# A 16-state scan shares its products between VectorE and GpSimd, and its output projection goes by tokens

## The chip, the cores and the metric

The kernel runs on one core of one Trainium2 chip. The metric is the device time of a run in microseconds (us), lower is better. The five engines are called as the profile calls them: PE (TensorE, with PEld for its weight loads), DVE (VectorE), ACT (ScalarE), POOL (GpSimd) and SP (SyncE, which here issues the DMAs).

## The reference

The model has two layers on an image tensor x of 4 images x 128 channels x 64 x 64 pixels. Layer 0 is what the change touches. Cut to that part:

```python
# order: pixels sorted by the score of their 4x4 patch; x_re: x in that order, tokens of 128 channels
xz = layernorm(x_re + pe_re) @ in_proj_w.T           # 4096 tokens an image, 512 columns
xm, z = xz[..., :256], xz[..., 256:]
xc = silu(causal_conv4(xm) + conv1d_b)
dt_low, Bc, Cc = split(xc @ x_proj_w.T)              # 8, 16 and 16 columns
dt = softplus(dt_low @ dt_proj_w.T + dt_proj_b)
dA  = exp(dt[..., None] * A)                         # per token: 256 channels x 16 states
dBx = dt[..., None] * Bc[:, :, None, :] * xc[..., None]
def step(h, inp):                                    # over the 4096 tokens
    dA_t, dBx_t, C_t = inp
    h = dA_t * h + dBx_t
    return (h, einsum('bds,bs->bd', h, C_t))
y = (ys + D * xc) * silu(z)
out_m = y @ out_proj_w.T                             # back to 128 channels
x = x + out_m put back in the pixels' own order
```

Layer 1 is a scan with 256 states over the tokens (as they stand in the image, 8 chunks of 512 an image), and a spectral convolution. It reads layer 0's result and takes most of the time, but no instruction of it changes except from where it reads the projected tokens of the last image.

## The kernel before, in words

The kernel has three parts in time. `layer0_front` sorts the pixels and writes the normalised tokens, already in order, to DRAM (xnt), and the sorting permutation (permd). `layer0_scan` is the 16-state scan and ends with layer 0's result x2. `layer1` is the rest.

**Tiling of the scan.** An image's 4096 tokens are cut into 8 units of PJ = 512 tokens, so there are 32 units. The 256 channels are two halves (k) on 128 partitions, tokens run along the free dimension. A unit is scanned in two sub-blocks (i) of SUB = 256 tokens, and the 16 states in 8 pairs (g). One step j is one pair of states over one sub-block: a tile of 128 partitions x (2 states x 2 halves x 256 tokens) = 128x1024. There are 16 steps a unit and 512 in all. What is carried from a sub-block to the next is the last state of each of the rows (`last`), folded into the first token of the next sub-block's input.

**One step j** consists of these instructions, line numbers of the kernel before:

- `fetch` (L518): two DMAs on SP bring the rows of B and C for the two states, broadcast to 128 partitions (tile bc, named bcb in the profile; 6 buffers).
- `carry` (L527, every fourth step): POOL multiplies the first factor of the sub-block by `last`.
- `spread` (L532): POOL makes v = dx * B (128x1024), and L537 adds the carried value to the first token of v (128x4). v has 4 buffers.
- `lift` (L546): ACT makes the factors f = exp(dt * A) by four instructions, into one of two buffers in PSUM.
- `scan` (L554): DVE runs the recurrence over f and v and writes `states`, one buffer in PSUM. L558: DVE multiplies the states by C into p (3 buffers). L559: DVE copies the last states (128x4) to `last`.
- `add_up` (L570): PE adds p to y in PSUM by two matmuls with the identity; after the last pair of a sub-block, two matmuls with a diagonal matrix add D * xc (L576).
- `gated` (L586): once a sub-block, DVE multiplies y by silu(z) into yg.

**The order** is written by hand: no scheduler moves anything, and each engine runs its own instructions in the order in which the program names them. The loop over j stands at L632 to L649. In iteration j it issues fetch for step j+5, carry and spread for j+3, lift for j+1, the gate of step j-2 where a sub-block has ended there, scan of j with its product and copy, and add_up for j-1. So v is made three steps ahead of its scan, and f one step ahead.

**Work beside the steps.** `project` makes a unit's xz, dt, dx, and the B and C rows, which go through DRAM (bcd) to be broadcast; `output` projects a gated unit back to 128 channels; `put_back` sorts an image back and adds it to x. They are generators that yield after each piece: "mm" is a piece of matmuls that takes the one PSUM buffer `mm`, "post" the instruction that empties it, "free" a piece that needs no such buffer. `beside(j)` runs once an iteration, after add_up: at most one matmul piece holds the buffer at a time, and the projection goes ahead of the output. Projection of unit n starts when j reaches 16(n-1)-9, that is 25 steps before the unit's first scan.

**Output before.** A unit's 512 tokens are projected in four rounds (L457 to L468). Matmuls work on 32 rows at a time (every sixteenth token, so that a row is a patch), and ACT copies 32x512 into a tile `om` that holds a whole image in SBUF. After an image's last unit, `put_back` is queued behind the output and takes om back by matmuls with the permutation (L482), eight rounds, DVE adding each to the image tile xs (L488); xs holds half an image, loaded when that half begins, and is stored when it ends. The last image is not put back here: om goes to DRAM (omd, L655), and layer 1 puts it back at its beginning, reading omd at L989.

**Where layer 1 begins.** Its first loads (dlb, L1284, on SP) come behind the store of omd. Its scan (L1314, DVE) runs in place in SBUF over a ring buffer which POOL fills (L1298), with factors in PSUM from ACT (L1310).

Of the kernel before, what the change touches and what calls it, by code (L numbers as in the profile page):

```python
# [337 lines left out]
def layer0_scan(ctx: ExitStack, tc, ident, w, x, xnt, permd, x2, omd, psum, following):  # L338
# [111 lines left out]
    def output(b, unit, yg):  # L450

        if unit == 0:
            oms[b] = big.tile([128, 2, 16, 128], F32, tag="om", name="om", bufs=1)
        om = oms[b]
        yr = yg.rearrange("p k (r o) -> p k o r", o=16)
        rows = bass.ts(unit % 4, 32)
        for o in range(0, 16, 4):  # L457
            yield "mm"
            ps = middle()
            for i in range(4):  # L460
                for k in range(2):
                    nc.tensor.matmul(  # L462
                        ps[rows, bass.ts(i, 128)], yr[:, k, o + i, :], ow[:, k, :], start=k == 0, stop=k == 1
                    )
            yield "post"
            nc.scalar.copy(  # L466
                om[rows, unit // 4, o : o + 4, :], ps[rows].rearrange("p (i c) -> p i c", i=4)
            )  # L468

    def put_back(b):  # L470

        om = oms.pop(b)
        for h in range(2):
            xs = sm.tile([128, 8, 4, 64], F32, tag="xs", name="xs")
            cols = bass.ts(h, L // 2)
            nc.sync.dma_start(xs.rearrange("c py oy x -> c (py oy x)"), x[b][:, cols])
            for oy in range(4):
                yield "mm"
                ps = middle()
                for ox in range(4):  # L480
                    for r in range(2):
                        nc.tensor.matmul(  # L482
                            ps[:, bass.ts(ox, 128)], om[:, r, 4 * oy + ox, :], perm_t[:, b, r, bass.ts(h, 128)],
                            start=r == 0, stop=r == 1,
                        )
                yield "post"
                dst = xs[:, :, oy, :].rearrange("c py (px ox) -> c py px ox", ox=4)
                nc.vector.tensor_tensor(  # L488
                    dst, dst, ps.rearrange("c (ox py px) -> c py px ox", ox=4, px=16), ALU.add
                )  # L490
            nc.sync.dma_start(x2[b][:, cols], xs.rearrange("c py oy x -> c (py oy x)"))

# [11 lines left out]
    def tiles():  # L504
        return (
            big.tile([128, 4, PJ], F32, tag="xz", name="xz", bufs=3),
            big.tile([128, 2, PJ], F32, tag="dt", name="dt", bufs=3),
            big.tile([128, 2, PJ], F32, tag="dx", name="dx", bufs=3),
            big.tile([128, PJ // SUB, NS, 2], F32, tag="af", name="af"),
            dr.tile([2, NS, PJ], F32, tag="bcd", name="bcd"),  # L510
        )

    def fetch(j):
        n, i, g = place(j)
        bc = wk.tile([128, 2, 2, SUB], F32, tag="bc", name="bcb", bufs=6)
        src = ready[n][4][:, 2 * g : 2 * g + 2, bass.ts(i, SUB)]
        for q in range(2):
            nc.sync.dma_start(bc[:, q], src[q].partition_broadcast(128))  # L518
        return bc
# [9 lines left out]
    def spread(j, bc):  # L529
        n, i, g = place(j)  # L530
        v = wk.tile([128, 2, 2, SUB], F32, tag="v", name="v", bufs=4)
        nc.gpsimd.tensor_tensor(  # L532
            v, ready[n][2][:, :, bass.ts(i, SUB)].unsqueeze(1).broadcast_to((128, 2, 2, SUB)),
            bc[:, 0].unsqueeze(2).broadcast_to((128, 2, 2, SUB)), ALU.mult,
        )
        if units[n][1] or i:
            nc.gpsimd.tensor_tensor(  # L537
                v[:, :, :, 0], v[:, :, :, 0], ready[n][3][:, i, 2 * g : 2 * g + 2, :], ALU.add
            )
        return v  # L540
# [9 lines left out]

    def scan(j, v, bc):
        n, i, g = place(j)
        flat = "p n k t -> p (n k t)"
        nc.vector.tensor_tensor_scan(  # L554
            states.rearrange(flat), factors[j % 2].rearrange(flat), v.rearrange(flat), 0.0, ALU.mult, ALU.add
        )
        p = wk.tile([128, 2, 2, SUB], F32, tag="p", name="p")
        nc.vector.tensor_tensor(p, states, bc[:, 1].unsqueeze(2).broadcast_to((128, 2, 2, SUB)), ALU.mult)  # L558
        nc.vector.tensor_copy(last[:, 2 * g : 2 * g + 2, :], states[:, :, :, SUB - 1])  # L559
        return p  # L560
# [20 lines left out]
    def gated(j):  # L581
        n, i, g = place(j)
        if i == 0:
            ygs[n] = big.tile([128, 2, PJ], F32, tag="yg", name="yg")
        cols = bass.ts(i, SUB)
        nc.vector.tensor_tensor(ygs[n][:, :, cols], y.pop((n, i)), ready[n][0][:, 2:4, cols], ALU.mult)  # L586
        if i == PJ // SUB - 1:
            b, unit = units[n]
            behind.append(output(b, unit, ygs.pop(n)))
            if unit == L // PJ - 1 and b < NB - 1:  # L590
                behind.append(put_back(b))

# [7 lines left out]

    ready, ygs, oms, behind = {0: tiles()}, {}, {}, []
    for _ in project(*units[0], ready[0]):
        pass
    fronts, extra, rear, holder = [], [], None, None
    ahead = [1]

    def beside(j):
        nonlocal rear, holder
        if holder:
            keep = holder.kind == "hold"  # L610
            holder.next()
            holder = holder if keep else None
        if ahead[0] < len(units) and j >= per * (ahead[0] - 1) - 9:
            ready[ahead[0]] = tiles()
# [6 lines left out]
        if (rear is None or rear.kind is None) and behind:  # L621
            rear = Work(behind.pop(0))
        for work in (*fronts, rear, *extra):
            if work and work.kind == "free":
                work.next()
        for work in (*fronts, rear, *extra):
            if work and work.kind == "mm" and holder is None:
                work.next()
                holder = work

    bcs, vs, prods = {}, {}, {}
    for j in range(-9, steps):  # L632
# [8 lines left out]
        if j < 0:  # L641
            beside(j)
            continue
        if j >= 2 and (j - 2) % pairs == pairs - 1:
            gated(j - 2)
        prods[j] = scan(j, vs.pop(j), bcs.pop(j))
        if j:
            add_up(j - 1, prods.pop(j - 1))
        beside(j)  # L649
    add_up(steps - 1, prods.pop(steps - 1))  # L650
    gated(steps - 1)
    while holder or extra[0].kind or rear and rear.kind or behind:
        beside(steps)
    for h in range(2):
        nc.sync.dma_start(omd[h], oms[NB - 1][:, h])  # L655

# [249 lines left out]
def layer1(ctx: ExitStack, tc, ident, weights, work, psum, second, phi, pqd, mud, x, omd, permd, first, x2, x3, out):  # L906
# [43 lines left out]
    def put_back():  # L950
# [3 lines left out]
        for h in range(2):  # L954
            for oy in range(4):
                om = wide().rearrange("p r (i c) -> p r i c", i=4)
                for r in range(2):
                    nc.sync.dma_start(om[:, r], omd[r][:, bass.ts(oy, 4)])
                perm = small()[:, 0:256].rearrange("p (r j) -> p r j", r=2)
# [544 lines left out]
def conv_attn_hybrid(ctx: ExitStack, tc, w, out):  # L1504
# [13 lines left out]
    permd = dram.tile([128, NB, 2, 256], F32, name="permd")  # L1518
    omd = dram.tile([2, 128, 16, 128], F32, name="omd")
    layer0_front(tc, ident, half, w, x, xnt, permd, pqd, mud)  # L1520
# [55 lines left out]
```

## Time and profile before

The median of 3 runs is 21105.47 us (21103.82 to 21108.15).

| what | us |
|---|---|
| profiled execution, whole | 21106.96 |
| span from its first to its last instruction | 21105.0 |
| before the first scan of layer 0 | 614.8 |
| 16-state scan, first scan to last gate | 2066.5 |
| from there to layer 1's first scan | 29.2 |
| layer 1, from its first scan to the end | 18394.5 |

| engine | busy us in the span | share | instructions |
|---|---|---|---|
| PE | 17551.7 | 83% | 99112 |
| DVE | 20433.2 | 97% | 11824 |
| ACT | 15761.0 | 75% | 28195 |
| POOL | 19751.2 | 94% | 3541 |

How to read it: times are of one execution. A row of a group of instructions names the line, the engine, the operation, the tile written and the tiles read, partitions x elements, and the count; then the busy time of all and the mean of one in ns; then the time in which the engine sat idle just before them, and what ended most of that time. A row of a wait names who waited for whom, the total, how often, and the longest. In a list in order of time, the first number is the start in us from the beginning of the span and the second the duration. Durations of neighbours overlap slightly, so the distance between two starts is the better measure of what an instruction costs its queue. PE's ends are modelled.

### The profile page before, as it was taken

What the parts mean: (1) busy time and instruction counts of PE and PEld (TensorE: products, weight loads), DVE (VectorE), ACT (ScalarE), POOL (GpSimd) and SP (SyncE); (2) the same over time, 40 slices, a digit from 0 to 9 for tenths busy, and PEclk for the clock granted to TensorE, in tenths of its full rate; (3) what the DMA queues carried; (4) which work ended last, traced back from release to release, by engine and by line L of the source; (5) the groups of instructions that cost most, each with busy time, mean ns of one, the idle gap of its engine ahead of it and who ended that gap; (6) DMA issues with size and microseconds to landing.
All of it is one profiled execution on the core that took longest, in us unless ns stands there. A gap on an engine that the chain in (4) does not pass through costs nothing.

```text
span 21105.0 us, 282109 instructions
## 1 busy us (share of the span) xinstructions
PE 17551.7 (83%) x99112; PEld 7740.7 (37%) x99112; DVE 20433.2 (97%) x11824; ACT 15761.0 (75%) x28195; POOL 19751.2 (94%) x3541
## 2 busy tenths in 40 slices
PE   7788844655858888877868999599999999999998
PEld 4344421322323333343323344243434434434434
DVE  7799999999999999999999999999999999999997
ACT  3667667777777777777777777787887777788876
POOL 2666699999999999999999999999999999999997
PEclk8999966776979999998979999699999999999999
DMA  1555554555656666665656777577777777777775
GB/s 69 133 142 143 145 162 156 183 174 172 219 174 224 222 226 224 222 211 196 210 186 223 231 239 238 173 238 236 238 235 232 235 234 235 237 235 233 232 231 182
DMA packets 2194842, 4287.94 MB, mean 203 GB/s; under 512 B 768744, under 2 KB 1288208, under 8 KB 1928080
## 3 DMA queue, kind: packets, MB, share of 16 engines
q1 hardware_dynamic: 2193424, 4269.90, 63.3%
q8 instruction: 784, 12.85, 0.2%
q14 instruction: 634, 5.19, 0.1%
HBM read 3645.09 MB, written 623.91 MB: 202 GB/s over the span
## 4 chain that ended last, share of the span: by engine, by line
DVE 51%; issue 15%; PE 12%; POOL 5%; ACT 4%; DMA 1%; DVEq 0%; SPq 0%; POOLq 0%; ACTq 0%
DVE ring L1314 49%; PE conv L1257 6%; POOL ring L1298 4%; PE yp L1344 3%; ACT da L1310 2%; PE fin L1199 1%; ACT conved L1269 1%; DMA strip<-in_phi 0%; ACT t L804 0%; PE mm L883 0%; PE mm L877 0%; PE mm L868 0%; PE mm L1039 0%; PE conv L1111 0%; ACT ye L1351 0%
## 5 line engine op out<-in xcount | busy, mean ns | idle before, releaser
L1298 POOL TENSOR_TENSOR ring<-u,dlb 128x4088 f32<-128x4088 f32 x2048 | 18075.4, 8889 | 67.4 <-DMA dlb<-delta 37.7
L1314 DVE TENSOR_TENSOR_SCAN ring<-da,ring 128x1024 f32<-128x1024 f32 x8192 | 17927.7, 2263 | 180.4 <-ACT da L1310 149.6
L1310 ACT ACTIVATE da<-dlb,at 128x511 f32<-128x511 f32 x16384 | 11321.1, 691 | 4049.2 <-DVE ring L1314 3763.3
L1257 PE MATMUL conv<-strip,tok 128*128 128x512 f32 (+3 forms) x20224 | 8569.6, 551 | 46.0 <-DMA strip<-in_phi 45.0
L1344 PE MATMUL yp<-ring,c 128*32 128x256 f32 x65536 | 4917.1, 428 | 2493.9 <-DVE ring L1314 1283.8
L1257 PEld LDWEIGHTS conv<-strip,tok 128*128 128x128 f32 x20224 | 3606.1, 191 | 4105.8 <-issue 3722.3
L1344 PEld LDWEIGHTS yp<-ring,c 128*32 128x32 f32 x65536 | 2007.5, 119 | 6188.5 <-issue 3468.9
L532 POOL TENSOR_TENSOR v<-dx,bcb 128x1024 f32<-128x1024 f32 x512 | 1208.8, 2361 | 633.0 <-DVE states L554 629.4
L1199 PE MATMUL fin<-conved,pq 128*128 128x512 f32 (+1 forms) x3840 | 1750.5, 549 | 9.2 <-ACT sum L1220 4.8
L546 ACT ACTIVATE f<-dt,an 128x255 f32<-128x255 f32 x2048 | 974.7, 476 | 493.0 <-DVE states L554 442.3
L554 DVE TENSOR_TENSOR_SCAN states<-f,v 128x1024 f32<-128x1024 f32 x512 | 1176.0, 2297 | 106.3 <-ACT f L546 54.7
L1351 ACT COPY ye<-yp 128x512 f32<-128x512 f32 x2048 | 1185.9, 579 | 24.5 <-PE yp L1344 23.4
L570 PE MATMUL y<-p,ident 128*128 128x512 f32 x2048 | 1008.6, 618 | 173.5 <-DVE p L558 170.0
L1269 ACT COPY conved<-conv 128x512 f32<-128x512 f32 x1664 | 963.0, 579 | 146.3 <-PE conv L1257 143.2
L1199 PEld LDWEIGHTS fin<-conved,pq 128*128 128x128 f32 x3840 | 644.5, 192 | 385.8 <-issue 278.0
L558 DVE TENSOR_TENSOR p<-states,bcb 128x1024 f32<-128x1024 f32 x512 | 627.0, 1225 | 38.3 <-DVE states L554 0.5
L570 PEld LDWEIGHTS y<-p,ident 128*128 128x128 f32 x2048 | 363.6, 193 | 709.1 <-issue 336.8
L1304 ACT COPY ring<-vf 128x8 f32<-128x8 f32 x2048 | 386.8, 189 | 4.1 <-DMA omd<-om 4.1
L462 PE MATMUL mm<-ow,yg 128*32 128x128 f32 x2048 | 250.8, 276 | 39.2 <-ACT om L466 37.7
L462 PEld LDWEIGHTS mm<-ow,yg 128*32 128x32 f32 x2048 | 219.3, 133 | 136.4 <-ACT om L466 60.8
L1357 ACT COPY last<-ring 128x8 f32<-128x8 f32 x1792 | 267.2, 198 | 0.0
L407 PE MATMUL mm<-xin,taps 128*128 128x512 f32 x512 | 236.4, 605 | 23.2 <-DVE f L384 20.0
(242 smaller groups left out, 5484.3 us busy)
## 6 DMA issues: line engine op xcount, KB each, us to landing
dlb<-delta SPq DMA_DIRECT2D x2048, 1024.0 KB, 5.3
strip<-in_phi SPq DMA_DIRECT2D x1536, 448.0 KB, 5.0
yd<-ye SPq DMA_DIRECT2D x2048, 256.0 KB, 4.6
bcb<-bcd SPq DMA_DIRECT2D x1024, 256.0 KB, 4.3
strip<-in_phi SPq DMA_DIRECT2D x1024, 256.0 KB, 4.9
pq<-pqd SPq DMA_DIRECT2D x1408, 64.0 KB, 4.4
yt<-yd SPq DMA_DIRECT2D x4096, 4.0 KB, 4.4
pq<-pqd SPq DMA_DIRECT2D x256, 128.0 KB, 4.2
```

The lines of the kernel that those rows point to most:

```text
L532: nc.gpsimd.tensor_tensor(v, ready[n][2][:, :, bass.ts(i, SUB)].unsqueeze(1).broadcast_to((128, 2, 2, SUB)), bc[:, 0].unsqueeze(2).broadca ...
L546: nc.scalar.activation(factors[j % 2][:, a, k, 1:], ready[n][1][:, k, SUB * i + 1 : SUB * i + SUB], AF.Exp, scale=an[:, k, 2 * g + a : 2 * ...
L554: nc.vector.tensor_tensor_scan(states.rearrange(flat), factors[j % 2].rearrange(flat), v.rearrange(flat), 0.0, ALU.mult, ALU.add)
L570: nc.tensor.matmul(t.rearrange("p k t -> p (k t)"), ident, p[:, a].rearrange("p k t -> p (k t)"), start=g == 0 and a == 0, stop=False, ski ...
L1199: nc.tensor.matmul(fin[:, bass.ds(c0, w)], pq[:, n, :], u[:, bass.ds(c0, w)], start=begin and n == 0, stop=end and not partly, skip_group_ ...
L1257: nc.tensor.matmul(ps[:, skip:], tok[:, 1 - r if side else r, j, :], strip[:, bass.ds(c0 - lo, TS - skip)], start=which == 0 and j == js[0 ...
L1269: nc.scalar.copy(u[:, cols], ps[:, cols])
L1298: nc.gpsimd.tensor_tensor(ring[:, q % NQ, :, :, 1:], ready[0][:, :, 1:].unsqueeze(1).broadcast_to((128, VD, 2, TS - 1)), dl[:, :, 1:].unsq ...
L1310: nc.scalar.activation(da[:, h, 1:], dl[:, d % VD, 1:], AF.Exp, scale=at[:, h, d : d + 1])
L1314: nc.vector.tensor_tensor_scan(v, da.rearrange("p h t -> p (h t)"), v, 0.0, ALU.mult, ALU.add)
L1344: nc.tensor.matmul(yp[i // 2][bass.ts(p, 32), i % 2], c[:, h, t], moving(h, 128 * i + 32 * p, 32), start=h == 0, stop=h == 1,)
L1351: nc.scalar.copy(ye, yp[j].rearrange("p i d t -> p i t d"))
```

## The change

All of it lies in `layer0_scan`, apart from a shape of omd.

- On 5 of 16 steps (pairs 1, 3, 5 of a unit's first sub-block and 1, 4 of its second) the step is "shared": the scan runs in place in v in SBUF, and one iteration later POOL copies its last states and makes its product with C, into a tile of its own (pp, 2 buffers). PE adds such a product three iterations after its scan instead of one. The other 11 steps are as before.
- In an iteration, POOL's queue now holds carry and v for j+3, then the copy and product of a shared j-1. The gate of j-2 moves from before the scan of j to after it and its product.
- bc has 8 buffers instead of 6, v 6 instead of 4, af and bcd 3 instead of 2.
- `output` takes a unit in one round: four groups of 128 tokens, 128x128 each, one ACT copy of 128x512 to a tile ot, and one store to omd in DRAM, which now holds all four images. om no longer stays in SBUF.
- `put_back` is a queue of its own beside the output, and takes the image in eight pieces; image rows and projected tokens of the next piece are loaded one piece ahead, and each piece is stored at once.
- A unit's projection starts 29 steps before its first scan instead of 25.
- Layer 1 reads omd[b, r] for the last image.

```diff
     def output(b, unit, yg):
-        if unit == 0:
-            oms[b] = big.tile([128, 2, 16, 128], F32, tag="om", name="om", bufs=1)
-        om = oms[b]
-        yr = yg.rearrange("p k (r o) -> p k o r", o=16)
-        rows = bass.ts(unit % 4, 32)
-        for o in range(0, 16, 4):
+        yield "mm"
+        ps = middle()
+        for i in range(PJ // 128):
+            for k in range(2):
+                nc.tensor.matmul(
+                    ps[:, bass.ts(i, 128)], yg[:, k, bass.ts(i, 128)], ow[:, k, :], start=k == 0, stop=k == 1
+                )
+        yield "post"
+        ot = sm.tile([128, PJ // 128, 128], F32, tag="ot", name="ot", bufs=2)
+        nc.scalar.copy(ot, ps.rearrange("p (i c) -> p i c", c=128))
+        rows = omd[b].rearrange("h r o c -> (h r o) c")[bass.ts(unit, PJ)]
+        nc.sync.dma_start(rows.rearrange("(i p) c -> p i c", p=128), ot)
...
+        def load(i):
+            h, oy = divmod(i, 4)
+            xs = sm.tile([128, 8, 64], F32, tag="xs", name="xs", bufs=2)
+            nc.sync.dma_start(xs, image(x, h, oy))
+            om = sm.tile([128, 2, 4, 128], F32, tag="om", name="om", bufs=2)
+            for r in range(2):
+                nc.sync.dma_start(om[:, r], omd[b, r][:, bass.ts(oy, 4)])
+            return xs, om
...
+    def shared(j):
+        n, i, g = place(j)
+        return g in ((1, 3, 5), (1, 4))[i]
+
-    def scan(j, v, bc):
+    def scan(j, v):
         n, i, g = place(j)
         flat = "p n k t -> p (n k t)"
+        h = v if shared(j) else states
         nc.vector.tensor_tensor_scan(
-            states.rearrange(flat), factors[j % 2].rearrange(flat), v.rearrange(flat), 0.0, ALU.mult, ALU.add
+            h.rearrange(flat), factors[j % 2].rearrange(flat), v.rearrange(flat), 0.0, ALU.mult, ALU.add
         )
-        p = wk.tile([128, 2, 2, SUB], F32, tag="p", name="p")
-        nc.vector.tensor_tensor(p, states, bc[:, 1].unsqueeze(2).broadcast_to((128, 2, 2, SUB)), ALU.mult)
-        nc.vector.tensor_copy(last[:, 2 * g : 2 * g + 2, :], states[:, :, :, SUB - 1])
+        return h
+
+    def keep(j, h):
+        n, i, g = place(j)
+        engine = nc.gpsimd if shared(j) else nc.vector
+        engine.tensor_copy(last[:, 2 * g : 2 * g + 2, :], h[:, :, :, SUB - 1])
+
+    def product(j, h, bc):
+        mine = shared(j)
+        p = wk.tile([128, 2, 2, SUB], F32, tag="pp" if mine else "p", name="p", bufs=2 if mine else 3)
+        engine = nc.gpsimd if mine else nc.vector
+        engine.tensor_tensor(p, h, bc[:, 1].unsqueeze(2).broadcast_to((128, 2, 2, SUB)), ALU.mult)
         return p
...
-        if ahead[0] < len(units) and j >= per * (ahead[0] - 1) - 9:
+        if ahead[0] < len(units) and j >= per * (ahead[0] - 1) - 13:
...
+        if j and shared(j - 1):
+            h = states_of.pop(j - 1)
+            keep(j - 1, h)
+            prods[j - 1] = product(j - 1, h, bcs.pop(j - 1))
+        h = scan(j, vs.pop(j))
+        if shared(j):
+            states_of[j] = h
+        else:
+            prods[j] = product(j, h, bcs.pop(j))
+            keep(j, h)
         if j >= 2 and (j - 2) % pairs == pairs - 1:
             gated(j - 2)
-        prods[j] = scan(j, vs.pop(j), bcs.pop(j))
-        if j:
+        if j >= 3 and shared(j - 3):
+            add_up(j - 3, prods.pop(j - 3))
+        if j and not shared(j - 1):
             add_up(j - 1, prods.pop(j - 1))
         beside(j)
```

## The prediction

> **What bounds the kernel now.** I read the page first, for where the time lies; then the busy time of each engine in the stretches between the layers; then the groups of instructions and the waits inside the layer-0 scan; and last single instructions in order of time, because what is to be added up is the distance between two starts and not the recorded durations, which overlap a little.
>
> The stretches (busy us of each engine, count of instructions, granted clock, DMA share, GB/s):
>
> ```profile
> 614.80:2681.30 2066.50, 1740.04 (x5561) 836.47 (x5560) 1890.43 (x1638) 1438.98 (x2712) 1387.11 (x1141) 0.98 0.54 141
> 2681.30:2710.50 29.20, 7.81 (x64) 6.86 (x64) 0.87 (x5) 5.20 (x9) 9.15 (x3) 0.73 0.36 144
> 2710.50:21000.00 18289.50, 15290.10 (x91936) 6595.91 (x91936) 18119.91 (x9036) 14074.61 (x25036) 18213.22 (x2283) 0.92 0.66 215
> ```
>
> The columns of busy time are PE, PE's weight load, DVE, ACT, POOL. The 16-state scan is the first stretch: 2066.5 us from its first scan to its last gate. DVE is busy 1890 of it, POOL only 1387. The third stretch is layer 1: POOL is busy in 18213 of 18290 us there and the change leaves its instructions alone, so I keep it as it is and only shift it. The gain or loss is made in the first two stretches.
>
> Inside the first stretch (count | busy us, mean ns | idle just before, releaser):
>
> ```profile
> L532 POOL TENSOR_TENSOR v<-dx,bcb 128x1024 f32<-128x1024 f32 x508 | 1199.5, 2361 | 632.9 <-DVE states L554 629.4 <-DMA bcb<-bcd 3.6
> L554 DVE TENSOR_TENSOR_SCAN states<-f,v 128x1024 f32<-128x1024 f32 x512 | 1176.0, 2297 | 106.3 <-ACT f L546 54.7
> L558 DVE TENSOR_TENSOR p<-states,bcb 128x1024 f32<-128x1024 f32 x512 | 627.0, 1225 | 38.3 <-DVE states L554 0.5
> L537 POOL TENSOR_TENSOR v<-v,af 128x4 f32<-128x4 f32 x480 | 96.9, 202 | 37.6
> L559 DVE COPY last<-states 128x4 f32<-128x4 f32 x512 | 77.6, 152 | 0.0
> DVE yg L586 <- PE y L576: 54.8, 38, 2.9
> DVE states L554 <- ACT f L546: 54.7, 33, 48.2
> DVE xs L488 <- DMA xs<-in_x: 23.7, 6, 7.6
> ```
>
> POOL's idle time is 633 us and ends with DVE's scan; DVE's own idle time is small: 55 us for y, 24 us for the image tile, and 6.5 us for f (48.2 of the 54.7 is the one wait at the start). So DVE sets the pace of this stage and POOL waits for it. One step, in order of time (start us, duration us), and POOL back to back, and layer 1's scan:
>
> ```profile
> 698.07 2.30 DVE L554 TENSOR_TENSOR_SCAN states<-f,v 128x1024 f32<-128x1024 f32 x1
> 700.46 1.22 DVE L558 TENSOR_TENSOR p<-states,bcb 128x1024 f32<-128x1024 f32 x1
> 701.60 0.15 DVE L559 COPY last<-states 128x4 f32<-128x4 f32 x1
> 701.88 2.30 DVE L554 TENSOR_TENSOR_SCAN states<-f,v 128x1024 f32<-128x1024 f32 x1
> ...
> 1002.89 2.35 POOL L441 TENSOR_TENSOR dx<-dt,xz 128x1024 f32<-128x1024 f32 x1
> 1005.20 2.35 POOL L532 TENSOR_TENSOR v<-dx,bcb 128x1024 f32<-128x1024 f32 x1
> 1007.63 0.20 POOL L537 TENSOR_TENSOR v<-v,af 128x4 f32<-128x4 f32 x1
> 1007.82 2.37 POOL L532 TENSOR_TENSOR v<-dx,bcb 128x1024 f32<-128x1024 f32 x1
> ...
> 5020.25 17.55 DVE L1314 TENSOR_TENSOR_SCAN ring<-da,ring 128x1024 f32<-128x1024 f32 x8
> ```
>
> A DVE step costs 3.81 us: 2.39 scan, 1.14 product, 0.28 copy. The sum for the stage now: 512 x 3.81 = 1951; 64 gates, each putting 0.66 in the place of 0.28, 24; 24 image additions at 0.59, 14; idle 86. Together 2075 against 2066 measured, 0.4% over.
>
> **The change, part by part.**
>
> *DVE loses 160 products and 160 copies* (5 of 16 steps, 32 units). A shared step leaves only its scan, which now runs in place in v. Layer 1 has the same scan (factors in PSUM, 1024 elements in place in SBUF): 17.55/8 = 2.19 us from start to start. New DVE sum: 352 x 3.81 = 1341; 160 x 2.19 = 350; 64 gates now behind a shared scan at 0.59, 38; image additions 14; total 1743 us before waits.
>
> *POOL gains them.* The product has no row on POOL, but v (L532) has the same shape, two SBUF inputs, one of them broadcast: 2.31 us from start to start when nothing depends on it (dx at 1002.89 to v at 1005.20), 2.44 when the next instruction reads it. I take 2.33; the ends are 2.31 and 2.44. The copy of 128x4 has no POOL row either; nearest is L537 of the same size at 0.20; the ends are DVE's 0.15 and 0.35. Nothing excludes that it is cheaper than I take it; at no cost at all it is 32 us less. POOL's queue for all units from the first shared product on (v 0 to 5 are made ahead in the six buffers while DVE waits for its first f): 480 v with their addition at 2.61 (1005.20 to 1007.82) = 1253; 26 without it at 2.31 = 60; 120 carries at 0.20 = 24; 31 dx at 2.31 = 72; 160 products at 2.33 = 373; 160 copies at 0.20 = 32. Total 1814 us, 70 more than DVE's 1743. **POOL becomes the bound of the stage**, at about 57.3 us a unit instead of 64.4.
>
> Here the Trainium skill speaks against the edit: "GPSIMD Engine Reference", section 4.1, wants elementwise work on VectorE, since a two-input operation is about twice as slow on GpSimd. The rows agree on the price (2361 against 1225 ns, 1.93 times). By the rule alone the move adds 160 x 1.14 = 181 us of engine time, and a kernel whose engines took turns would end near 21290. But these two run side by side and POOL has 633 us to spare in this stage, so the longer queue decides, not the sum.
>
> *Waits that the change adds.* (1) POOL's copy and product of step j-1 stand behind v of step j+3 and wait for scan j-1; behind them stand the next v, which DVE needs three steps later. With POOL as the bound DVE has by then got to about step j+2, so it may lag by some three steps (10 us) before POOL waits. (2) PE adds a shared product two steps later (j-3 in iteration j); behind it stand the next additions and the projection's matmuls, for which ACT's copies, then f behind them, then DVE wait. When POOL is just in time, the product of group 5 is ready 2.5 us after scan 9 starts, and two additions (1.8 each) and the diagonal pair (0.9) make the gate wait until about 7 us after that start, where DVE would be there after 2.2: a stall of up to 4.7 us twice a unit. It makes DVE lag, and the lag makes the next such stall shorter; DVE has 70 us over the stage, 2.2 a unit, for it. (3) SP's new stores of ot wait for ACT, the image loads for the store of the tile before (now up to 5.3 us at one load); behind them stand the fetches of bc, which with eight buffers are issued some four steps before POOL uses them (14 us, landing takes 4.3). I take 0.3 us a unit, 10 us, for all POOL waits; the ends are 0 and 2 us a unit (64).
>
> *Waits that go.* The gate stands behind one more scan (2.2 us; the longest of the 54.8 us of waits was 2.9), and image tiles are loaded ahead (23.7 us). Both were on DVE, which no longer bounds, so they are worth nothing by themselves; without them DVE's sum would be too close to POOL's.
>
> *Output projection:* per unit 16 records of 128x128 in place of 64 (a batch of 16 takes 1.9 us either way, L462 and L482), one copy in place of four (0.58 each), one more store of 256 KB, and 32 loads and stores an image in place of 4. PE and ACT have room (1740 and 1439 of 2066). It shows only at the end: now four rounds of matmul and copy, 2.63 us apart, stand between the last gate and the store that layer 1's first load waits for; one is left: 3 x 2.63 = 7.9 us less.
>
> *29 instead of 25 steps ahead:* silu with its two table loads (4.5 us of ACT) now falls on step 10 of 16, where the steps around it are full ones; there ACT's f was late by 0.17 us in the trace, and I count 1 us a unit of DVE's lag, hidden under POOL.
>
> **The sum.** The first shared scan ends 6.2 us after the first scan starts (3.81 + 2.39, at 614.8), so POOL's queue runs from 621 to 2435 if it never waits. The last v is ready 2.5 us earlier, at 2432; from the last scan's start to the gate it is 6.56 us as now (2674.68 to 2681.24), and one more product in PE's queue adds some 2: gate at 2440.5 instead of 2681.2, 241 less. With 8 less behind it and 10 for POOL's waits: 239 us. The span goes from 21105.0 to 20866, the profiled execution from 21106.96 to 20868; the median of the runs, 21105.47, is 1.5 us below it: **20866 us**, 1.1% faster.
>
> **Rivals.**
>
> *Waits between the engines eat a part.* For it: two queues within 4% of each other, joined by PE in order and by ACT's two buffers of f. Against it: three steps of slack each way. At 2 to 3 us a unit on POOL instead of 0.3, 54 to 86 us: 20920 to 20952.
>
> *POOL is quicker than summed and DVE bounds.* DVE's 1743 plus 20 to 40 us of waits would put the last gate at 2378 to 2398, 303 to 283 earlier than now: 20794 to 20814 with the 8 at the end. It needs POOL's product and copy at no more than 2.3 us together, and v's rows say 2.53.
>
> *Slower: the in-place scan locks POOL out.* The Trainium skill, "SBUF — State Buffer", section "The single rule", gives DVE and GpSimd a shared port that one of them holds for the whole instruction. Shared scans now write SBUF instead of PSUM; if POOL stood still for each, 160 x 2.19 = 350 us would be added to the bounding queue: 21105 - 239 + 350 = 21216. It decides from 239/160 = 1.5 us a shared step. Against it stand layer 1's rows: the same scan in SBUF at 2.19 us beside a POOL that is busy 99.6% of that stretch, at 8889 ns for 4088 elements, 2.17 ns each, where v in this stage has 2361/1024 = 2.31. The page too counts inputs from SBUF, and the scan has one of its two in PSUM.
>
> *The change doesn't do what it says* (POOL's product ends up waiting for DVE each time, and the pace stays 3.81 a step) would give about 21097, only the 8 us at the end. The code puts v three steps ahead of it, so I give it little.
>
> **Chances and range.** As summed: 0.62, with its own range 20845 to 20890 (copy 0.15 to 0.3, product 2.31 to 2.44, POOL waits 0 to 0.7 us a unit). Waits eat a part: 0.21. DVE bounds: 0.09. No change: 0.02. Slower: 0.06. What a measurement can tell from no change is 0.2%, 42 us, so the first three are faster: 0.92; same 0.02; slower 0.06. For 8 in 10 I leave out the slower cases, the upper end of the waits and the last of the DVE case: 20825 to 20945.
>
> **What would show it.** POOL busy over 95% of the scan stage, and its idle time no longer for DVE's scan; DVE's scan waiting for POOL's addition to v (L546 of the new kernel) instead; POOL's product at 2.3 to 2.4 us and its copy near 0.2; the shared scans at 2.2 to 2.3; a unit of 57 to 58 us; the stage some 240 us shorter, and layer 1 as long as it is (18394 us from its first scan to the end). Wrong would be: POOL's v or product longer than 2.5 us beside the in-place scans, POOL idle for DVE, PE or ACT by more than 2 us a unit, or a longer layer 1.

## The result and the profile after

The changed kernel takes 21222.28 us (median of 4 runs, 21218.0 to 21234.8) against 21105.26 us before: a ratio of 1.0056, 95% interval 1.0044 to 1.0069. It is **slower by 117 us** where 239 us less were predicted. The profiled execution took 21220.3 us, its span 21218.5.

The stretches of the changed kernel, cut as before: first scan to last gate, last gate to layer 1's first work, layer 1 (start:end, length, then busy us and count of PE, PE's weight load, DVE, ACT, POOL, the granted clock, DMA share, GB/s):

```profile
608.20:2805.80 2197.60, 1687.88 (x4076) 756.99 (x4076) 1667.04 (x1318) 1387.64 (x2619) 1758.28 (x1460) 0.88 0.50 142
2805.80:2835.00 29.20, 1.86 (x16) 1.59 (x14) 11.55 (x9) 9.12 (x15) 19.81 (x4) 0.62 0.39 153
2835.00:21100.00 18265.00, 15292.08 (x91904) 6598.85 (x91904) 18096.91 (x9027) 14061.63 (x25016) 18198.74 (x2282) 0.92 0.66 216
```

The scan stage takes 2197.6 us instead of 2066.5: 131.1 more. It begins 6.6 us earlier (608.2), and layer 1's first scan comes 18.5 us behind the last gate instead of 29.2, so 10.7 less. From that scan to the end it is 18394.2 us, as before (18394.5). 131.1 - 6.6 - 10.7 = 113.8, which is the difference of the two spans within 0.3. So all of the loss is in the scan stage, and there no engine bounds any more: outside its recorded work DVE has 531 us and POOL 439.

The groups of that stretch (count | busy us, mean ns of one | idle of the engine just before them, releasers):

```profile
L541 POOL TENSOR_TENSOR v<-dx,bcb 128x1024 f32<-128x1024 f32 x507 | 1193.0, 2354 | 165.2 <-DMA bcb<-bcd 165.0
L568 DVE TENSOR_TENSOR_SCAN states<-f,v 128x1024 f32<-128x1024 f32 x352 | 807.5, 2294 | 312.7 <-ACT f L555 272.4 <-POOL v L541 18.1 <-POOL last L576 2.8
L582 POOL TENSOR_TENSOR p<-v,bcb 128x1024 f32<-128x1024 f32 x160 | 375.9, 2350 | 0.0
L568 DVE TENSOR_TENSOR_SCAN v<-f,v 128x1024 f32<-128x1024 f32 x160 | 365.0, 2281 | 89.6 <-ACT f L555 80.6 <-POOL v L546 6.1 <-POOL af L536 2.9
L576 POOL COPY last<-v 128x4 f32<-128x4 f32 x160 | 30.2, 189 | 80.9 <-DVE v L568 80.9
```

The prices were right: POOL's product 2350 ns, its copy 189, the scan in place 2281, and v no slower than before (2354 against 2361). What is new is the third column: DVE waits for ACT's factors f (272.4 + 80.6 us, where it was 54.7). The waits of the same stretch (total us, times, longest; "SPq" is the DMA queue of SP):

```profile
DVE states L568 <- ACT f L555: 272.4, 96, 46.3
ACT xz L412 <- PE mm L407: 204.8, 58, 11.9
POOL v L541 <- DMA bcb<-bcd: 165.0, 89, 10.1
PE mm L407 <- DMA xin<-xnt: 155.6, 27, 11.0
DVE yg L609 <- PE y L599: 125.7, 31, 4.3
POOL dx L441 <- ACT dt L439: 91.1, 30, 4.0
DVE v L568 <- ACT f L555: 80.6, 28, 3.0
...
SPq L428 <- ACT bc L427: 524.1, 31, 17.5
SPq L463 <- ACT f L555: 275.2, 30, 12.2
```

Read from below, they are a chain. SP stands for ACT before it may store the projected tokens (L463; the row names f, but in the unit below the store leaves at 2077.49, just as ACT's copy of 2076.88 ends). PE's convolution taps (L407) then wait for the projection's input xin, ACT's xz (L412) for those taps, f stands behind xz on ACT, and DVE waits for f. Before, the taps waited for xin for 0.9 us in the whole stage. One unit in order of time (start us, duration, and in brackets the idle time of the engine before it and its releaser; SP, then PE, ACT, DVE):

```profile
2077.49 0.36 SPq L463 DMA_DIRECT2D omd<-ot  x1
...
2079.03 0.45 SPq L399 DMA_DIRECT2D xin<-xnt  x1
...
2074.89 1.95 PE L456 MATMUL mm<-ow,yg 128*128 128x128 f32 x16
2076.68 3.60 PE L593 MATMUL y<-p,ident 128*128 128x512 f32 x8
2086.06 5.14 PE L407 MATMUL mm<-xin,taps 128*128 128x512 f32 x8 [5.79 <-DMA xin<-xnt]
2094.48 3.60 PE L407 MATMUL mm<-xin,taps 128*128 128x512 f32 x8
...
2076.88 0.59 ACT L461 COPY ot<-mm 128x512 f32<-128x512 f32 x1 [2.40 <-PE mm L456]
2091.24 0.69 ACT L412 ACTIVATE xz<-mm,cb 128x512 f32<-128x512 f32 x1 [3.92 <-PE mm L407]
...
2093.92 2.30 DVE L568 TENSOR_TENSOR_SCAN states<-f,v 128x1024 f32<-128x1024 f32 x1 [1.25 <-ACT f L555]
2104.12 0.69 DVE L609 TENSOR_TENSOR yg<-y,xz 128x512 f32<-128x512 f32 x1 [4.33 <-PE y L599]
```

The output's matmuls at 2074.89 feed ACT's copy at 2076.88; its store leaves SP at 2077.49, and only behind it can xin be issued (2079.03) of a projection whose matmuls PE has next. PE has nothing to do for 5.79 us, and the eight taps after that gap take 5.14 us instead of 3.60. The next additions to y start that much later, and the gate at 2104.12 waits 4.33 us for them. With 29 steps a projection begins one iteration behind the output's store; with 25 it begins five behind it.

From every second gate to the next (the second of each unit) it was 62.4 to 63.9 us before in a unit with nothing of put_back beside it. After, most are 66 to 69 (the first ones up to 71.9), those with put_back up to 78.4, and the last two, which have no projection of layer 0 left beside them, 56.5 and 50.5. POOL's predicted 57.3 us is reached only there.

### The profile page after: what moved, and what is told of

It reads as the page before. It is cut to its first block, busy times and chain, and to the rows that moved or that the text cites. A ratio compares the mean times of both kernels' runs of the same rounds, so it can differ in the third digit from the quotient of the medians.

```text
span 21218.5 us, 278713 instructions
## 1 busy us (share of the span) xinstructions
PE 17494.9 (82%) x97576; PEld 7657.8 (36%) x97576; DVE 20208.9 (95%) x11504; ACT 15707.8 (74%) x28099; POOL 20123.7 (95%) x3861
## 4 chain that ended last, share of the span: by engine, by line
DVE 52%; issue 15%; PE 12%; ACT 4%; POOL 4%; DMA 1%; DVEq 0%; SPq 0%; POOLq 0%; ACTq 0%
DVE ring L1348 51%; PE conv L1291 6%; POOL ring L1332 3%; PE yp L1378 3%; ACT da L1344 2%; PE fin L1233 1%; ACT conved L1303 1%; DMA strip<-in_phi 0%; PE mm L911 0%; PE mm L902 0%; ACT t L838 0%; PE conv L1145 0%; ACT ye L1385 0%; PE mm L1073 0%; PE mm L917 0%
## 5 line engine op out<-in xcount | busy, mean ns | idle before, releaser
L541 POOL TENSOR_TENSOR v<-dx,bcb 128x1024 f32<-128x1024 f32 x512 | 1204.6, 2354 | 165.3 <-DMA bcb<-bcd 165.0
L593 PE MATMUL y<-p,ident 128*128 128x512 f32 x2048 | 1047.8, 656 | 201.6 <-DVE p L582 110.3
L568 DVE TENSOR_TENSOR_SCAN states<-f,v 128x1024 f32<-128x1024 f32 x352 | 807.5, 2294 | 312.7 <-ACT f L555 272.4
L593 PEld LDWEIGHTS y<-p,ident 128*128 128x128 f32 x2048 | 406.6, 206 | 761.1 <-issue 473.1
L582 DVE TENSOR_TENSOR p<-states,bcb 128x1024 f32<-128x1024 f32 x352 | 431.0, 1224 | 24.0 <-DVE states L568 0.4
L568 DVE TENSOR_TENSOR_SCAN v<-f,v 128x1024 f32<-128x1024 f32 x160 | 365.0, 2281 | 89.6 <-ACT f L555 80.6
L407 PE MATMUL mm<-xin,taps 128*128 128x512 f32 x512 | 287.5, 714 | 191.4 <-DMA xin<-xnt 175.3
L582 POOL TENSOR_TENSOR p<-v,bcb 128x1024 f32<-128x1024 f32 x160 | 375.9, 2350 | 0.0
L441 POOL TENSOR_TENSOR dx<-dt,xz 128x1024 f32<-128x1024 f32 x32 | 75.2, 2349 | 245.6 <-ACT dt L439 245.6
```

Source lines behind the costliest of these rows:

```text
L541: nc.gpsimd.tensor_tensor(v, ready[n][2][:, :, bass.ts(i, SUB)].unsqueeze(1).broadcast_to((128, 2, 2, SUB)), bc[:, 0].unsqueeze(2).broadca ...
L568: nc.vector.tensor_tensor_scan(h.rearrange(flat), factors[j % 2].rearrange(flat), v.rearrange(flat), 0.0, ALU.mult, ALU.add)
L593: nc.tensor.matmul(t.rearrange("p k t -> p (k t)"), ident, p[:, a].rearrange("p k t -> p (k t)"), start=g == 0 and a == 0, stop=False, ski ...
```

## The experiments

Each kernel was run in a batch beside the kernel before (21100.46, 21105.08 and 21102.26 us for the three batches). All but the last are single runs. Several runs of one kernel spread over 12 us (before) to 28 us (the last experiment), so smaller differences count only where a line of the trace stands beside them. Theory A puts the loss on the projection's new place among the in-order queues; its rival B on the shared steps and the coupling of DVE and POOL.

**e1_noshare: no step is shared**, everything else as after.

```diff
     def shared(j):
-        return g in ((1, 3, 5), (1, 4))[i]
+        return False
```

> The changed kernel with no shared step: all products and copies are DVE's again; output by tokens, the place of the projection 29 steps ahead, the buffers and the moved gate stay. Theory A (the new placement and the new store close a ring of in-order queues: the unit's input xin is loaded by SP behind the store of ot, which waits for ACT's copy, which waits for PE; PE then stands idle for xin, ACT behind PE, DVE behind ACT's f): PE still waits for xin, over 60 us in all, but a full step of 3.81 us leaves ACT slack, so 21060 to 21150. Theory B (the shared steps take the slack that silu and softplus on ACT need, wherever the projection stands): without sharing no stall is left, 62.4 us a unit, 21020 to 21050, and PE's wait for xin costs nothing.

21183.13 us. Outside of both ranges, but the loss stays without a shared step: 83 us slower than before, ordinary units mostly of 65 to 68 us. PE waits 96.3 us for xin and POOL 440 us for bc. That speaks against B as the cause, and says that at 29 steps sharing costs 39 us more.

**e2_place25: the projection starts 25 steps ahead as before**, everything else as after.

```diff
-        if ahead[0] < len(units) and j >= per * (ahead[0] - 1) - 13:
+        if ahead[0] < len(units) and j >= per * (ahead[0] - 1) - 9:
```

> The changed kernel with the projection 25 steps ahead again, four steps behind the output's store instead of one; all else as changed. Theory A: PE's wait for xin (155 us in the stage) falls below 40, the stalls that follow it (some 5.4 us of the 68.4 a unit) go: 21050 or less, down to 20900 if the rest of the ring opens too. Theory B: silu and softplus only meet other steps, their stalls of some 8 us a unit move and stay: 21150 to 21250.

21020.34 us: **this one number turns 117 us of loss into 80 us of gain.** Its waits and its row of the scan stage (same columns as above):

```profile
DVE v L568 <- ACT f L555: 139.7, 36, 11.3
DVE states L568 <- ACT f L555: 107.3, 40, 48.2
DVE yg L609 <- PE y L599: 52.5, 31, 4.5
PE mm L407 <- DMA xin<-xnt: 46.2, 6, 11.6
POOL v L541 <- DMA bcb<-bcd: 164.0, 53, 11.7
...
608.00:2600.50 1992.50, 1615.96 (x4078) 725.81 (x4077) 1664.57 (x1318) 1388.79 (x2622) 1751.39 (x1460) 0.92 0.56 156
```

xin keeps PE waiting 6 times instead of 27, y 52.5 us instead of 125.7, f 247 instead of 353 (48.2 of both is about the wait at the start). Most ordinary units take 57.1 to 58.8 us, about POOL's predicted bound of 57.3. The nine units with put_back beside them take 65.5 to 77.8, together some 113 us more than ordinary ones; the six waits for xin lie there. POOL's waits for bc are as long in all as in after (164 and 165 us), so they did not make the difference.

**e3_xin_early: 29 steps, but xin of the next unit is loaded at the end of the projection before it.**

```diff
-        xin = big.tile([128, 3 + PJ], F32, tag="xin", name="xin")
-        nc.sync.dma_start(xin, xnt[b][:, bass.ds(PJ * unit, 3 + PJ)])
+        xin = xins.pop((b, unit), None)
...
+        if n < NB * L // PJ:
+            xins[divmod(n, L // PJ)] = fetch_x(*divmod(n, L // PJ))
```

> The changed kernel with xin of a unit loaded some seven steps earlier, at the end of the projection before it, so that it is there when PE wants it; the projection's place and the store stay. Theory A: PE's wait for xin goes to nearly zero and 5.4 us a unit with it, more in the units where an image is put back: 20980 to 21060. Theory B: PE waits less, DVE waits for f as long as before (353 us in all, within 60): 21170 to 21220.

21074.26 us, 148 less than after and just above A's range. PE's wait for xin is gone and y falls to 35.3 us, but f stays at 304 of 353, as B had it:

```profile
DVE states L579 <- ACT f L566: 226.9, 83, 48.0
DVE v L579 <- ACT f L566: 77.5, 27, 3.2
DVE yg L620 <- PE y L610: 35.3, 12, 5.5
```

So loading early is worth 148 us, and of DVE's waits it takes 90 us off y and 49 off f; most of the waits for f at 29 steps have another cause.

**e5_store_act: 29 steps, ot is stored by ACT's queue instead of SP's.**

```diff
-        nc.sync.dma_start(rows.rearrange("(i p) c -> p i c", p=128), ot)
+        nc.scalar.dma_start(rows.rearrange("(i p) c -> p i c", p=128), ot)
```

> The changed kernel with the store of ot issued by ACT, right behind its copy, instead of SP; all else as changed. Theory A: SP no longer waits for ACT there (275 us of waits), xin is issued some 4 us earlier a unit: 21060 to 21130, since xin still comes only a step ahead. Theory B: no change, 21200 to 21240.

21100.87 us, in A's range: 121 less than after. The store behind which xin stood is the same knot as in e3, opened from its other end; on ACT it costs 0.37 us of issue. PE still waits 7 times for xin, but for the first time only in the units of put_back.

**e6_noshare25: no shared step and 25 steps**, which completes a square with e1, e2 and after.

> The changed kernel with the projection 25 steps ahead and no shared step, so output by tokens, buffers and the moved gate alone. If the placement was the loss and sharing a gain: DVE sets the pace at 62.4 us a unit without its waits for y, and the ends are 18 us shorter: 21030 to 21110, at least 20 above the run with the placement alone taken back (21020). If sharing itself loses something even there: below 21010.

21115.24 us, 5 above the range.

| us | shared steps | none shared |
|---|---|---|
| 29 steps ahead | 21222 (after) | 21183 (e1) |
| 25 steps ahead | 21020 (e2) | 21115 (e6) |

**Sharing gains 95 us at 25 steps and loses 39 at 29**; the place costs 68 us without sharing and 202 with it. The two edits do not add: what sharing gains depends on the other engines keeping POOL's pace.

**e4_share_only: the kernel before with the shared steps alone** (output in four rounds, om in SBUF, 25 steps, the gate behind the scan; put_back a queue of its own; bc with 7 and v with 5 buffers, one less of each than after).

```diff
+    def shared(j):
+        return g in ((1, 3, 5), (1, 4))[i]
...
+        if j and shared(j - 1):
+            h = states_of.pop(j - 1)
+            keep(j - 1, h)
+            prods[j - 1] = product(j - 1, h, bcs.pop(j - 1))
```

> The kernel before with the shared steps alone: output in four rounds, om in SBUF, put_back and the projection 25 steps ahead as before; for want of SBUF bc has 7 buffers and v 5. If POOL's sum is what bounds a unit with shared steps, 57 to 59 us a unit away from put_back, and the units beside it as before, some 17 us over three units: 20900 to 20960. If the four rounds of output stand in the way of the shared additions on PE: 21000 or more.

21046.89 us: 55 us faster than before, and "21000 or more" held. A unit takes 60.6 to 62 us where e2 has 57.1 to 58.8; DVE waits 263 us for f, 48.1 of them at the start, and ACT 108 us for PE at the om copies of the old output. So in an ordinary unit (63.2 us before, on average) the sharing alone gains less than 2 us, where e2 gains some 5, though e2's total is only 27 us lower: put_back takes back in e2 much of what its ordinary units gain. How much of this is the four rounds and how much the missing buffers was not tested apart.

**e7_place25_xin, e8_load_later, e9_stores_act: what keeps put_back's units long.** e7 is e2 with xin loaded as in e3. e8 is e7 with put_back's loads of the next piece issued later, behind the two pieces that need no PSUM buffer. e9 is e8 with ot and both rows of bcd stored by ACT's queue.

```diff
-            (xs, om), ahead = ahead, load(i + 1) if i < 7 else None
+            xs, om = ahead
             yield "free"
             yield "free"
+            ahead = load(i + 1) if i < 7 else None
...
-        nc.sync.dma_start(bcd[0], bc[32 : 32 + NS, :])
-        nc.sync.dma_start(bcd[1], bc[64 : 64 + NS, :])
+        nc.scalar.dma_start(bcd[0], bc[32 : 32 + NS, :])
+        nc.scalar.dma_start(bcd[1], bc[64 : 64 + NS, :])
```

> Projection 25 steps ahead and xin loaded some seven steps early; shared steps as changed. The units without an image to put back run at 57 to 59 us already with the placement alone, those beside put_back at 68 to 78, 113 us too much in all. If late xin behind put_back's loads is the cause there (six waits, 46 us): 20950 to 20990. If it is the late fetches of bc (POOL waits 164 us for them): no better than 21000.

> The run before this, and put_back's load of the next piece issued two steps later, after the store of the tile that it overwrites has landed, so that SP doesn't stand still for it (87 us of SP's waits). If SP's standing there makes the fetches of bc late: another 30 to 60 us, 20900 to 20950. If not: within 15 of the run before.

> The run before this, and the stores of ot and of the B and C rows issued by ACT behind its own copies, so that SP never waits for ACT (560 us of its waits with the placement alone taken back). If SP's waits for ACT still cost: 20870 to 20910, the sum of POOL's queue. If they are hidden, ACT's three issues of 0.37 us a unit are all that is added: within 20 of the run before, either way.

20990.63, 20954.94 and 20935.45 us: 30, 36 and 20 us less, one after the other; the first lies on the edge of its range, the second 5 us above it. The units with put_back go from 67.9, 77.8, 68.1 (e2's first three) to 64.0, 72.2, 67.5, to 61.7, 65.0, 64.2, and to 60 to 63. All three edits take something off SP that stood for another's result with loads behind it: in e8, SP waits 59 us for the stored image pieces instead of 87, and POOL 94.5 us for bc instead of 144. The last edit takes the stores that wait for ACT off SP (those of bcd alone held it for 524 us in after). POOL's wait for bc falls from 94.5 to 28.9, but its wait for dx rises from 28.6 to 60.7, and the 20 us are within what single runs differ by; this fits the case "hidden" of the expectation, and not a pace of POOL's sum alone. The scan stage of e9:

```profile
DVE v L580 <- ACT f L567: 105.9, 42, 3.3
DVE states L580 <- ACT f L567: 96.6, 56, 48.2
POOL dx L449 <- ACT dt L447: 60.7, 29, 4.3
DVE yg L621 <- PE y L611: 34.5, 21, 3.4
POOL v L553 <- DMA bcb<-bcd: 28.9, 18, 4.0
...
608.00:2517.40 1909.40, 1590.95 (x4079) 717.96 (x4078) 1663.90 (x1318) 1393.52 (x2624) 1748.09 (x1459) 0.93 0.58 162
```

**e10_stores_act29 and e11_stores_act21: is the place of the projection still worth something when no queue is in its way?** Both are e9, with 29 and with 21 steps. In e11, put_back also begins seven iterations later (`range(10)` for `range(3)`), so that its loads come behind the tokens' stores.

```diff
-        if ahead[0] < len(units) and j >= per * (ahead[0] - 1) - 9:
+        if ahead[0] < len(units) and j >= per * (ahead[0] - 1) - 13:
```

> The last run (xin early, put_back's load later, stores by ACT) with the projection 29 steps ahead again. If the ring through SP was all that the placement did: 20925 to 20960, as with 25. If the placement also puts silu, softplus and the matmuls before them on steps where ACT and PE have no slack (2.9 and 4.8 us of DVE's waits for f in each unit of the changed kernel): 21000 to 21080.

> The same with the projection 21 steps ahead (and put_back's first load ten steps after the last gate, not three, since the output comes later). If only the distance to the output counts: as with 25, 20920 to 20960. If the steps on which silu and softplus fall count: different from it by more than 30, either way.

21036.27 and 21004.31 us: 101 and 69 us more than at 25 steps. In e10 no wait for xin is left and y costs 5.7 us in all, yet most ordinary units take 61.4 us, with f late at four places of each. DVE's waits for f in its scan stage:

```profile
DVE states L580 <- ACT f L567: 227.2, 85, 48.5
DVE v L580 <- ACT f L567: 74.5, 26, 3.0
```

That is 302 us, and 203 in e9: 99 us more, as much as the whole difference in time. Without shared steps it is the same: 168 us in e1 and 97 in e6, 70 us more for the 68 us of the square. One unit of e10 in order of time, some of ACT's instructions, then DVE's gate and its waits:

```profile
1968.71 0.59 ACT L426 COPY xz<-mm 128x512 f32<-128x512 f32 x1 [1.11 <-PE mm L424]
1969.31 1.28 ACT L428 ACT_TABLE_LOAD   x1
1970.61 1.91 ACT L428 ACTIVATE xz<-xz 128x2048 f32<-128x2048 f32 x1
1972.53 1.28 ACT L567 ACT_TABLE_LOAD   x1
1973.83 2.00 ACT L567 ACTIVATE f<-dt,an 128x255 f32<-128x255 f32 x4
...
1965.11 0.67 DVE L621 TENSOR_TENSOR yg<-y,xz 128x512 f32<-128x512 f32 x1
1975.93 2.29 DVE L580 TENSOR_TENSOR_SCAN v<-f,v 128x1024 f32<-128x1024 f32 x1 [2.87 <-ACT f L567]
1979.77 2.30 DVE L580 TENSOR_TENSOR_SCAN states<-f,v 128x1024 f32<-128x1024 f32 x1 [1.55 <-ACT f L567]
1990.15 2.30 DVE L580 TENSOR_TENSOR_SCAN states<-f,v 128x1024 f32<-128x1024 f32 x1 [2.88 <-ACT f L567]
2007.42 2.30 DVE L580 TENSOR_TENSOR_SCAN states<-f,v 128x1024 f32<-128x1024 f32 x1 [1.27 <-ACT f L567]
```

The first wait stands behind silu with its two table loads (4.52 us of ACT, 1969.31 to 1973.83), the third behind softplus with two more (3.66 us, 1984.40 to 1988.06). Together it is 8.6 us of waits in this unit. e9 issues the same work on ACT, and an ordinary unit of it waits 4.8 us for f:

```profile
957.10 2.30 DVE L580 TENSOR_TENSOR_SCAN states<-f,v 128x1024 f32<-128x1024 f32 x1 [0.82 <-ACT f L567]
970.53 2.29 DVE L580 TENSOR_TENSOR_SCAN v<-f,v 128x1024 f32<-128x1024 f32 x1 [3.31 <-ACT f L567]
973.50 2.30 DVE L580 TENSOR_TENSOR_SCAN states<-f,v 128x1024 f32<-128x1024 f32 x1 [0.68 <-ACT f L567]
```

There softplus costs 3.31 and silu only 0.82. So the price of silu is 0.82 us at one place and 2.87 at another. Short shared steps are not the reason, since in e1, where no step is shared, silu at the place of 29 steps costs as much (in e6, at 25 steps, 0.17 to 0.40 in ordinary units):

```profile
925.22 2.30 DVE L568 TENSOR_TENSOR_SCAN states<-f,v 128x1024 f32<-128x1024 f32 x1 [2.80 <-ACT f L555]
```

The traces show what the place is: a gate stands just in front of it. y has one buffer in PSUM, so PE's first additions of the next sub-block wait for the gate that reads it (0.76 us in this unit of e10). Behind them stands the last matmul that silu needs (L424), then ACT's copy of it (1968.71), silu, and the f that comes late. From the gate's start to the scan that waits for this f it is 10.82 us here (1965.11 to 1975.93), and 10.8 to 10.9 in nearly every unit of all five kernels at 29 steps, in e1 too; DVE has only two full steps to do meanwhile. At 21 steps the unit's other gate stands there: again 10.81 us (e11, 851.80 to 862.61), but DVE has only a full and a shared step to do and waits 4.42. At 25 steps silu comes five steps behind a gate, the distance is 22.2 us in e9, and ACT's copy in front of silu waits for nothing. No run moved that matmul alone, so this is read and not tested.

**e12_timed: the kernel of e9 in timed rounds.**

> The run with stores by ACT, 25 steps ahead, timed against the kernel before: 20935 within 10, ratio 0.992.

20939.05 us (median of 4 runs, 20916.33 to 20944.54) against 21102.26 before: ratio 0.9921, 95% interval 0.9904 to 0.9937. It beats the kernel before by 163 us and the changed one by 283.

## Why the prediction was wrong

It said 20866 us, faster; it is 21222. The 356 us between can be laid out by the runs: e9 is the changed kernel with SP's queue cleared and the projection back at 25 steps, and takes 20935.

| from | to | us |
|---|---|---|
| after 21222 | e10: queue cleared, 29 steps, 21036 | 186 |
| e10 21036 | e9: 25 steps, 20935 | 101 |
| e9 20935 | the sum, 20866 | 69 |

In the other order, the place first (after to e2: 202), the queue is worth 85. The two overlap by about a hundred, which fits that a projection that starts further from the output's store meets it less.

**The step that failed: "29 instead of 25 steps ahead."** It followed one piece, silu, to step 10, took from the trace of before that "there ACT's f was late by 0.17 us", and counted "1 us a unit of DVE's lag, hidden under POOL". The place costs 202 us over 32 units, 6.3 a unit. About half of it goes with the queue, by the store in front of xin (next paragraph). The half that e10 leaves is f coming late, 99 us more of it than in e9, with 2.87 us behind silu. The 0.17 us had been measured at another place: in the trace of before silu stands at step 14, and the late f is that of the next unit's step 0:

```profile
676.45 2.30 DVE L554 TENSOR_TENSOR_SCAN states<-f,v 128x1024 f32<-128x1024 f32 x1 [0.17 <-ACT f L546]
```

It was carried over to step 10 without following what silu waits for there: a matmul behind PE's additions, which wait for the gate. Softplus was not followed at all; with shared steps it keeps DVE waiting some 3 us a unit at all three places (3.31 in e9, 2.88 in e10, 3.07 in e11), and 0.30 in an ordinary unit of e6 without. And the cover did not reach: **"DVE has 70 us over the stage"** stood against 455 us in after (2197.6 less the 1743 of its own sum).

**"Waits that the change adds" (3)** listed the right store: SP's store of ot waits for ACT. It named the fetches of bc behind it, and those alone. Also behind it, one iteration away and only because of the new place, stands xin, which PE, not POOL, waits for. Every DMA of the moved projection had to be set against every new one on SP; the prediction dealt with the two edits in two paragraphs and put neither into the other's queue. e3 and e5 each take this one knot away, and gain 148 and 121 us.

**POOL's waits: "0.3 us a unit, 10 us"**, with 64 as the upper end. They were 394 us in after (bc 165, dx 91, the copies of last states 81, the carry 57), more than six times that end. By these rows, 229 us of that is POOL waiting for DVE and ACT; what made bc late was not taken apart. Yet at its best, in e9, the last gate is at 2517.3 where the sum with its 10 us has 2450: 67 us, 2.1 a unit, and POOL is busy for 92% of the stage, not the "over 95%" that was to show the forecast. That is what the first rival, "waits between the engines eat a part", put at 2 to 3 us a unit: its mechanism was right, and its size fits e9. In the changed kernel itself the place and the queue made these waits several times larger.

**"Waits that go"** counted y's 54.8 us as removed, since the gate stands behind one more scan. They rose to 125.7: the additions that the gate needs stand on PE behind taps which wait for xin and then run slowly. In e10, where nothing is in their way, they are 5.7. The step (2) of PE's order, a stall "of up to 4.7 us twice a unit", was near what a gate then waited (4.33), but for another reason.

**Right were** the prices (product 2.33 taken, 2.35 measured; copy 0.20 and 0.189), POOL's bound of 57.3 us a unit (57.1 to 58.8 in e2, 56.5 in a unit of after without projection), layer 1 unchanged to 0.3 us, and the tail (7.9 less taken, 10.7 measured).

**The rivals.** The in-place scan that locks POOL out was put at 21216, and the kernel takes 21222: a near hit for a mechanism that is not there. v and the product run at 2354 and 2350 ns beside it, the scan at 2281. The rule on one port for DVE and POOL ("SBUF — State Buffer" in the Trainium skill, section "Who interferes with whom") frees an instruction of DVE with at most one input from SBUF (outside its two-port modes), and the scan has one; these rows agree. That DVE bounds is refuted by its 455 us over its own sum, and that nothing changes by the 117 us. The rule against elementwise work on GpSimd holds here for the price alone: at 25 steps the move gains 95 us of the end.

What stays open is how much of the loss is PE's clock, which fell with the gaps, how the 69 us between e9 and the sum divide, and whether the gate in front of silu is all that makes 29 and 21 steps worse places than 25 once the queue is clear.

## What to carry to other kernels

Adding up each engine's queue gives a floor, and the best run came near it (e9's stage takes 1909 us, the sum has 1836 with its waits, 4% less); it says nothing of whether the other engines can keep that pace. For every step that is moved, write down each queue it issues to, the DMA queue first, and what stands next to it there at its new place: a load behind a store that waits for an engine makes a ring out of four queues. Follow a moved piece back as well, to what it waits for at its new place: here a gate stood there. Try a placement and an offload in all four combinations before either is judged, since here the one turned the other's gain into a loss.

## What was not expected of the hardware

After a gap PE runs slowly for some microseconds. In the changed kernel four additions (L593) behind a gap of 4.57 us took 3.78 us, and 1.98 without such a gap; the eight taps above took 5.14 us behind 5.79 us of idle time and 3.60 eight microseconds later. Over the scan stage the granted clock was 0.98 before, 0.88 after, 0.92 in e2 and 0.93 in e9; after and e9 run the same matmuls there, and PE is busy with them for 1688 us in the one and 1591 in the other. The Trainium skill, "TensorE: Matmul & The Clock Gate", section "Part 1: The HAM clock gate (the "warmup" mystery)", gives the rule: an idle window of about 3.4 us brings the clock down to half. The two gaps shown are longer than that and agree with it; where the limit lies the traces don't show, since four additions took 1.98 to 3.63 us behind gaps of 2.73 us in e6, and 1.98 behind one of 3.82 us in e9. What it means here is that a wait for a load is paid twice: by the gap, and by the slower matmuls behind it, for which ACT and the gate stand in line.
